# Program order for a product mixed with an attention pass, and a layernorm folded into the weights of the next layer

## The chip, the cores and the metric

The kernel runs on one core of one Trainium2 chip. The metric is device microseconds (us) of one execution; lower is better. Engines are named as in the profile: PE is TensorE, PEld its weight loads, DVE is VectorE, ACT is ScalarE, POOL is GpSimd.

## The reference, cut to what matters

Four graph layers on 4096 nodes with 128 features and one dense 4096x4096 adjacency; after each layer comes a residual sum and a layernorm.

```python
x = _layernorm(x + _L0_gnn_ref(x, adj, ...))   # signed attention
x = _layernorm(x + _L1_gnn_ref(x, adj, ...))   # Chebyshev filter, twice: four products adj @ (4096x128)
x = _layernorm(x + _L2_gnn_ref(x, adj, ...))   # attention with 4 heads of 32
x = _layernorm(x + _L3_gnn_ref(x, adj, ...))   # h @ W_self + (adj @ h / deg) @ W_neigh

# the attention of the third layer
tau = adj_t * exp(max(0.2 * C, C))             # C = alpha_src + alpha_dst, for each pair and head
att = tau / sum(tau)
z   = einsum('mnh,nhf->mhf', adj_t * att, h_prime)
```

The change concerns the fourth product of the Chebyshev layer, the attention, and the layernorm between the attention and the last layer.

## The kernel before: the parts concerned

The attention runs as eight passes (four windows of 1024 target nodes, two pairs of heads) of 32 steps, one step for each tile of 128 source nodes. A step needs three DVE and two POOL instructions and, on PE, two groups of four matmuls with 32 output columns each, one group for the softmax denominator (`den`) and one for the numerator (`num`):

```python
def step(self, nt, l2w, bufs, a, sq):
    E, D = self.E, self.D
    tau  = l2w.tile([P, 2, WB], F32, name="tau",  bufs=bufs[0])
    tau2 = l2w.tile([P, 2, WB], F32, name="tau2", bufs=bufs[1])
    nc.vector.scalar_tensor_tensor(tau[:, 0, :], D[0], E(nt, 0), a, op0=ALU.max, op1=ALU.mult)
    nc.gpsimd.tensor_tensor(tau2[:, 0, OWN:WB], tau[:, 0, OWN:WB], a[:, OWN:WB], ALU.mult)
    nc.vector.scalar_tensor_tensor(tau2[:, 0, 0:OWN], D[0][:, 0:OWN], E(nt, 0), sq, op0=ALU.max, op1=ALU.mult)
    nc.vector.scalar_tensor_tensor(tau[:, 1, :], D[1], E(nt, 1), a, op0=ALU.max, op1=ALU.mult)
    nc.gpsimd.tensor_tensor(tau2[:, 1, :], tau[:, 1, :], a, ALU.mult)
    return tau, tau2

def product(self, is_den, nt, r):
    # ... four matmuls into one accumulator, 32 of its rows each
    for h in range(2):
        for mb in range(2):
            q = 32 * (2 * h + mb)
            nc.tensor.matmul(acc[q:q + 32, :], weights(nt, 2 * self.hp + h, is_den),
                             r[:, h, mb * IB:(mb + 1) * IB], start=nt == 0, stop=nt == NT - 1)
```

The first pass is mixed with the fourth product. There the order on each engine is left to a scheduler:

```python
for ib in range(NB):
    p = ps_p.tile([P, IB], F32, name="pp")
    for c in range(NB):
        a = chunk(ld, adjT, ib, c)
        for k in range(TB):
            nc.tensor.matmul(p, w[:, c * TB + k, :], a[:, k, :], ...)
        if ib >= 2 and done < ready and (c % 2 or ready - done > TB):
            next(first_pass)
            done += 1
    # ... the chain of the block: add, elu, transpose, residual, statistics
    normalize_x(ib, ps_x, "px")
    sources_and_targets(ib)      # ends with four casts to bf16 on DVE
    ready += TB
for heads in first_pass:
    pass
```

The other seven passes stand in a part of the program whose order is kept as written. The last layer's layernorm was explicit, in front of its two products:

```python
nc.vector.tensor_scalar_add(s, mv[:, tb, 1], LN_EPS)
nc.scalar.activation(s, s, AF.Sqrt)
nc.vector.reciprocal(s, s)
nc.vector.scalar_tensor_tensor(m, mv[:, tb, 0], -1.0, s, op0=ALU.mult, op1=ALU.mult)
# eight times:
nc.scalar.activation(r, r, AF.Identity, bias=m[:, k:k + 1], scale=s[:, k:k + 1])
# then transpose, copy, multiply by W3, copy
```

One more line adds the residual to the last layer's own weights, at the very start and on POOL:

```python
nc.gpsimd.tensor_tensor(W3[:, 1, :], W3[:, 1, :], ident, ALU.add)
```

## Time and profile before

The time was 2312.57 us, the median of three runs (2310.97 to 2317.0). The profiled execution has a span of 2316.5 us, so it is one of the slower ones. The stages, by the starts of marker instructions in its trace (the first matmul of the fourth product, DVE's first addition of its last block, DVE's second step of the second pass, ACT's copy of the last `num`):

| stage | from | to | us |
|---|---|---|---|
| layer 0 and three products | 0 | 1100.7 | 1100.7 |
| fourth product, first pass mixed in | 1100.7 | 1420.0 | 319.3 |
| hand-over, up to the second step of the second pass | 1420.0 | 1460.9 | 40.9 |
| seven passes, up to the copy of the last `num` | 1460.9 | 2221.3 | 760.4 |
| tail: last block of the attention, rest of the last product, output | 2221.3 | 2316.5 | 95.2 |

Read such a table by asking, for each row, which engine is full. The lines that show it are in the prediction: PE in the second row, none in the third, DVE in the fourth. A microsecond taken from an engine that is not full in its row is worth nothing by itself.

### The profile page before, as it was taken

The page shows a single profiled execution, that of the slowest core. Times are in us where ns is not written, and L with a number is a line of the kernel's source. Part 1 is how long each engine was busy: PE and PEld are TensorE (multiplying, and loading weights), DVE is VectorE, ACT ScalarE, POOL GpSimd, SP SyncE. Part 2 cuts the span into 40 slices and gives each one's busy share as a digit, 9 for nine tenths or more (in the row PEclk, how much of TensorE's full clock was granted, in tenths as well). Part 3 has the DMA queues.
Part 4 walks back from the last instruction along what each step waited for, and adds up shares of the span by engine and source line. Part 5 has one row for each costly group of instructions (what it writes and reads, how often), then busy time and mean ns, then how long its engine had stood idle before and what let it go on. Part 6 is the DMA issues. An engine that isn't in the chain of part 4 may idle for free. (4 is left out here: it accounts for less than half of the span.)

```text
span 2316.5 us, 22706 instructions
## 1 busy us (share of the span) xinstructions
PE 2189.3 (95%) x8550; PEld 848.2 (37%) x8550; DVE 1235.3 (53%) x1789; ACT 609.3 (26%) x960; POOL 846.3 (37%) x541
## 2 busy tenths in 40 slices
PE   5899999999999999999999998768999999999998
PEld 3333444444444444444433332112222222222233
DVE  5454461000011010000167657899999999999955
ACT  5764100000000000000122121553364335334520
POOL 0000000000000000000043423898999899989930
PEclk9899999999999999999999999999999999999999
DMA  9785758888866767788866774344666566656665
GB/s 370 288 331 202 244 185 281 299 303 297 272 233 236 262 228 260 266 273 273 273 245 226 269 262 175 127 164 146 235 226 233 216 239 237 237 215 238 234 221 180
DMA packets 85336, 561.72 MB, mean 242 GB/s; under 512 B 9568, under 2 KB 15712, under 8 KB 17760
## 3 DMA queue, kind: packets, MB, share of 16 engines
q1 hardware_dynamic: 76928, 554.73, 68.0%
q10 hardware_dynamic: 8288, 5.44, 0.8%
q8 instruction: 69, 1.13, 0.2%
q14 instruction: 51, 0.42, 0.1%
HBM read 558.04 MB, written 2.10 MB: 242 GB/s over the span
## 5 line engine op out<-in xcount | busy, mean ns | idle before, releaser
L647 POOL TENSOR_TENSOR tau<-tau,chunk 128x1024 f32<-128x1024 f32 x256 | 611.0, 2387 | 79.8 <-DVE tau L646 71.8
L659 PE MATMUL den<-tau,cs 128*32 128x512 f32 x2048 | 392.9, 608 | 63.0 <-DVE tau L646 55.4
L601 POOL TENSOR_TENSOR x<-x,B2R 128x512 f32<-128x512 f32 x8 | 10.2, 1270 | 1208.5 <-DMA chunk<-in_adjT 1116.4
L659 PE MATMUL num<-tau,hc 128*32 128x512 f32 x2048 | 374.0, 599 | 4.7 <-POOL tau L647 4.0
L642 DVE SCALAR_TENSOR_TENSOR tau<-d,es,chunk 128x1024 f32<-128x1024 f32 x256 | 326.6, 1276 | 7.4 <-PE d L632 4.1
L646 DVE SCALAR_TENSOR_TENSOR tau<-d,es,chunk 128x1024 f32<-128x1024 f32 x256 | 327.1, 1278 | 0.1
L621 ACT ACTIVATE sq<-chunk 128x704 f32<-128x704 f32 x256 | 200.9, 791 | 410.3 <-DVE tau L644 317.3
L643 POOL TENSOR_TENSOR tau<-tau,chunk 128x320 f32<-128x320 f32 x256 | 226.5, 885 | 64.8 <-DVE tau L642 32.9
L644 DVE SCALAR_TENSOR_TENSOR tau<-d,es,sq 128x704 f32<-128x704 f32 x256 | 241.9, 945 | 13.3 <-PE num L659 9.7
L777 PE MATMUL pp<-chunk,w 128*128 128x512 f32 x512 | 235.6, 601 | 1.2 <-DVE t2T L783 1.2
L731 PE MATMUL pp<-chunk,xT 128*128 128x512 f32 x448 | 236.5, 630 | 0.0
L486 PE MATMUL pacc<-chunk,t 128*128 128x512 f32 x512 | 223.5, 592 | 0.0
L486 PE MATMUL pacc<-chunk,v 128*128 128x512 f32 x512 | 222.5, 592 | 0.0
L486 PE MATMUL pacc<-chunk,x 128*128 128x512 f32 x512 | 221.7, 593 | 0.0
L314 PE MATMUL pacc<-chunk,hw 128*128 128x512 f32 x408 | 197.0, 623 | 2.7 <-DVE hw L379 2.7
L659 PEld LDWEIGHTS den<-tau,cs 128*32 128x32 f32 x2048 | 64.0, 107 | 306.5 <-DVE tau L646 169.8
L659 PEld LDWEIGHTS num<-tau,hc 128*32 128x32 f32 x2048 | 91.3, 110 | 155.0 <-issue 138.3
L486 PEld LDWEIGHTS pacc<-chunk,v 128*128 128x128 f32 x512 | 97.2, 190 | 122.0 <-issue 122.0
L486 PEld LDWEIGHTS pacc<-chunk,x 128*128 128x128 f32 x512 | 96.5, 190 | 117.2 <-issue 117.2
L486 PEld LDWEIGHTS pacc<-chunk,t 128*128 128x128 f32 x512 | 96.1, 190 | 115.3 <-issue 115.3
L777 PEld LDWEIGHTS pp<-chunk,w 128*128 128x128 f32 x512 | 91.7, 190 | 125.8 <-issue 119.0
L533 DVE COPY w<-ptr 128x512 f32<-128x512 f32 x8 | 5.5, 692 | 241.5 <-PE ptr L103 241.5
(182 smaller groups left out, 1574.5 us busy)
## 6 DMA issues: line engine op xcount, KB each, us to landing
chunk<-in_adjT SPq DMA_DIRECT2D x386, 1024.0 KB, 4.9
chunk<-in_adj SPq DMA_DIRECT2D x128, 1024.0 KB, 4.8
keep<-in_adjT SPq DMA_DIRECT2D x13, 1024.0 KB, 5.0
xT<-in_xT ACTq DMA_DIRECT2D x8, 256.0 KB, 6.0
out<-o ACTq DMA_DIRECT2D x8, 256.0 KB, 3.6
W1A<-in_w1a ACTq DMA_DIRECT2D x1, 384.0 KB, 3.5
W1B<-in_w1b ACTq DMA_DIRECT2D x1, 384.0 KB, 4.3
W0T<-in_w0gT ACTq DMA_DIRECT2D x1, 64.0 KB, 5.3
```

What stands on the lines that cost most here:

```text
L314: nc.tensor.matmul(p, hw[:, j * TB + k, :], a[:, k, :], start=first and k == 0, stop=last and k == TB - 1)
L486: nc.tensor.matmul(p, stationary(c * TB + k), a[:, k, :], start=n == 0 and k == 0, stop=n == NB - 1 and k == TB - 1)
L601: nc.gpsimd.tensor_tensor(x[:, tb, :], x[:, tb, :], B2R[:, None, :].to_broadcast([P, TB, F]), ALU.add)
L621: nc.scalar.activation(sq, a[:, 0:OWN], AF.Square)
L642: nc.vector.scalar_tensor_tensor(tau[:, 0, :], D[0], E(nt, 0), a, op0=ALU.max, op1=ALU.mult)
L643: nc.gpsimd.tensor_tensor(tau2[:, 0, OWN:WB], tau[:, 0, OWN:WB], a[:, OWN:WB], ALU.mult)
L644: nc.vector.scalar_tensor_tensor(tau2[:, 0, 0:OWN], D[0][:, 0:OWN], E(nt, 0), sq, op0=ALU.max, op1=ALU.mult)
L646: nc.vector.scalar_tensor_tensor(tau[:, 1, :], D[1], E(nt, 1), a, op0=ALU.max, op1=ALU.mult)
L647: nc.gpsimd.tensor_tensor(tau2[:, 1, :], tau[:, 1, :], a, ALU.mult)
L659: nc.tensor.matmul(acc[q:q + 32, :], weights(nt, 2 * self.hp + h, is_den), r[:, h, mb * IB:(mb + 1) * IB], start=nt == 0, stop=nt == NT - 1)
L731: nc.tensor.matmul(p, y[:, (2 * mp + c) * TB + k, :], a[:, k, :], start=c == 0 and k == 0, stop=c == 1 and k == TB - 1)
L777: nc.tensor.matmul(p, w[:, c * TB + k, :], a[:, k, :], start=c == 0 and k == 0, stop=c == NB - 1 and k == TB - 1)
```

## The change

Its intent: keep the matmul groups of a step together in the mixed stage by writing the order down, let the first pass use the same buffers as the others so that the hand-over closes, and shorten the chain in front of the last product. The diff, cut to its core:

```diff
-    nc.gpsimd.tensor_tensor(W3[:, 1, :], W3[:, 1, :], ident, ALU.add)
+    def later_constants(psum, name):      # called inside layer 0; other constants moved here too
+        ...
+            nc.vector.tensor_tensor(W3[:, 1, :], W3[:, 1, :], ident, ALU.add)
+            nc.vector.memset(mean, 1.0 / F)
+            nc.tensor.matmul(pw, mean, W3..., start=True, stop=True)
+            nc.vector.tensor_sub(W3..., W3..., pw)      # weights without their column mean
 ...
-                nc.vector.tensor_copy(dv[:, blk], d)          # the four casts of the targets
+                nc.scalar.copy(dv[:, blk], d)
 ...
     def layer3_blocks(mp):
-                # statistics, -mean/sigma, eight normalisations, transpose, multiply, copy
+                # transpose x as it is; statistics beside it; multiply; 1/sigma as the copy's scale
+                            nc.scalar.activation(y[:, t, :], q[:, k, 0, :], AF.Copy, scale=scale)
+                            nc.scalar.activation(x[:, t, :], q[:, k, 1, :], AF.Copy, scale=scale)
 ...
-            with tc.tile_pool(name="l2a", ...):   # first pass, own buffers, order left to the scheduler
+            with tc.manual_schedule(engines={PE, DVE, Activation, Pool}):
+                for ib in range(NB):
+                    for c in range(NB):
+                        ...                                   # four matmuls of the fourth product
+                        if c == NB - 1:
+                            chains.append(block_end(ib, p))
+                        one(chains)                           # one segment of a block's chain
+                        if (c in (1, 3, 5, 6, 7) if ib > 2 else (ib, c) == (2, 7)) and ...:
+                            step()                            # one step of the first pass
+                while chains:                                 # the last block's chain between steps
+                    one(chains)
+                    step()
-                    tau, tau2 = heads.step(nt, l2w, (3, 4), a, sq)
+                    tau, tau2 = heads.step(nt, l2w, (3, 3), *ahead)
```

## The prediction

> **What bounds the kernel now.** I read four views in this order: the page's busy shares, the stretches of the run by stage, the order of matmuls inside the overlapped stage, and the vector engine's own order where one stage hands over to the next.
>
> ```profile
> span 2316.5 us, 22706 instructions
> PE 2189.3 (95%) x8550; PEld 848.2 (37%) x8550; DVE 1235.3 (53%) x1789; ACT 609.3 (26%) x960; POOL 846.3 (37%) x541
> ```
>
> The 95% of PE is an average over stages with different limits, so I cut the span by stage. The columns are length, PE, PEld, DVE, ACT, POOL busy, granted clock, DMA share, GB/s.
>
> ```profile
> 1100.00:1420.00 320.00, 316.44 (x1074) 121.42 (x1076) 177.16 (x286) 63.56 (x108) 102.92 (x63) 1.00 0.71 252
> 1420.00:1460.00 40.00, 27.42 (x118) 7.17 (x116) 28.02 (x43) 10.37 (x19) 15.81 (x10) 0.87 0.29 109
> 1460.00:2222.00 762.00, 701.39 (x4085) 200.62 (x4086) 758.33 (x759) 336.62 (x557) 726.45 (x461) 0.99 0.60 214
> 2222.00:2317.00 95.00, 81.32 (x220) 37.45 (x218) 41.69 (x177) 8.68 (x27) 0.00 (x0) 0.93 0.55 188
> ```
>
> Everything before 1100 is layer 0 and three products, PE-bound and hardly touched. Then come: the fourth product with the first attention pass mixed in (PE never idle); a hand-over of 40 us in which no engine is full; seven more passes, bound by DVE (758 of 762 us); and a tail. The change aims at the first two and shortens the chain in the last.
>
> In the mixed stage, the PE order counts. One 128x128 by 512 matmul shows as two records (x2), and four 32-column ones as x8:
>
> ```profile
> 1352.13 1.04 PE L659 MATMUL den<-tau,cs 128*32 128x512 f32 x2
> 1353.11 1.10 PE L591 MATMUL px<-xT,WD 128*96 128x512 f32 x2
> 1354.14 1.04 PE L659 MATMUL den<-tau,cs 128*32 128x512 f32 x2
> 1355.11 1.13 PE L777 MATMUL pp<-chunk,w 128*128 128x512 f32 x2
> 1356.17 1.05 PE L659 MATMUL den<-tau,cs 128*32 128x512 f32 x4
> 1357.15 2.84 PE L777 MATMUL pp<-chunk,w 128*128 128x512 f32 x6
> 1359.92 1.07 PE L659 MATMUL den<-tau,cs 128*32 128x512 f32 x8
> 1360.81 1.05 PE L659 MATMUL num<-tau,hc 128*32 128x512 f32 x8
> ```
>
> Read the starts. A whole group of four takes 0.89 us (1359.92 to 1360.81). But the scheduler split the group of 1352 into 1+1+2: 0.98, 0.97 and 0.98 us, 2.93 in place of 0.89. A whole step, den and num together, takes 1.86 us (1359.92 to 1361.78).
>
> At the hand-over, DVE starts of L642, L644, L646 make one step of pass two:
>
> ```profile
> 1449.72 1.27 DVE L646 SCALAR_TENSOR_TENSOR tau<-d,es,chunk 128x1024 f32<-128x1024 f32 x1
> 1454.40 1.28 DVE L642 SCALAR_TENSOR_TENSOR tau<-d,es,chunk 128x1024 f32<-128x1024 f32 x1 [3.41 <-PE d L632]
> 1458.86 0.95 DVE L644 SCALAR_TENSOR_TENSOR tau<-d,es,sq 128x704 f32<-128x704 f32 x1 [3.17 <-ACT sq L621]
> 1459.73 1.27 DVE L646 SCALAR_TENSOR_TENSOR tau<-d,es,chunk 128x1024 f32<-128x1024 f32 x1
> 1460.92 1.27 DVE L642 SCALAR_TENSOR_TENSOR tau<-d,es,chunk 128x1024 f32<-128x1024 f32 x1
> ```
>
> Two waits of over 3 us for the new pool's buffers and the second pass's targets. From 1460.92 on a step takes 3.24 us of DVE (1.19 + 0.86 + 1.19 start to start) and the engine does not rest again.
>
> **What the Trainium skill says.** "TensorEngine Tiling (Array Packing)", Key Properties: different tiles can load weights and multiply in parallel, and a change of tiling mode drains the engine. The trace agrees on the first: x8 and x4 and x2 all take about 0.9 to 1.0 us. "SBUF — State Buffer", Who interferes with whom: a vector instruction in a two-port mode (casts, copies, tensor_scalar), or one with two SBUF inputs against a reading GpSimd instruction, waits for the whole other instruction. The trace agrees here:
>
> ```profile
> L597 DVE CAST dv<-elu_r x8: 417/2480/2507, 1147.4 to 1440.5; 32x512 bf16<-32x512 f32 x8
> L700 DVE SCALAR_TENSOR_TENSOR mean<-mv,rstd x4: 166/2014/2318, 1596.2 to 2228.6; 128x8 f32<-128x8 f32 x4
> ```
>
> Both (minimum/median/maximum ns) are cheap when GpSimd is idle and take about one 2.4 us GpSimd multiply otherwise. "ScalarE: Activation LUTs", What ACT_TABLE_LOAD costs: about 1283 ns for a load and 93 ns for each pointer operand of an ACTIVATE. The trace has 1283 for the load; the second I need for the new scaled copies.
>
> **The change part by part.** (1) Program order in the mixed stage. Work is the same; the groups of four stay whole (the built order shows den x4, num x4 always together). A block without steps takes 31.24 us before (first matmul sums at 1128.54 and 1159.78), of which 0.85 is a wait for its one accumulator, so 30.4. The last three blocks with four steps each take 42.12, so (42.12 - 30.4)/4 = 2.9 us a step where 1.86 would do. In the new order: block 0 27.7; block 1 30.4; block 2 30.4 + 1.3 for the targets; block 3 30.4 + 8.4 + 1 (5 den, 4 num; 1 for a transposition that waits for the normalisation); blocks 4 to 6 30.4 + 5x1.86 + 1 = 40.7 each; block 7 30.4 + 3x1.86 + 1 = 37.0. The sum is 288.7, so the product ends at 1100.7 + 288.7 = 1389, against 1420. But it holds 24 steps instead of about 28.
>
> (2) The hand-over. Eight steps of the first pass are left, with the last block's chain between them. DVE: 2.7 us to the activation's end and 4.5 to the normalised block (1419.99 to 1422.69 to 1427.19 before), 8x3.24 = 25.9, 1.0 for the products with cs, about 4 for small waits and the next targets. That is 38: the second pass begins at 1427 and its second step at 1431, against 1460.92. Gain of (1) and (2) about 30 us; I take 28, since in program order each chain segment can hold an engine up.
>
> (3) The targets' casts move from DVE to ACT, which has 256 us idle there: inside (1) and (2). The last block's targets are now built in the DVE-bound stage: two subtractions of 0.7 us, each liable to a GpSimd wait, so 2 us lost.
>
> (4) Buffers: tau2 goes from 4 to 3. L644 of step s+1 then needs the num of step s-2. In the steps at 2204 to 2216 that num ends 1.9 to 2.4 us before L644 starts, so it fits, except where a transposition or the two-layer product of the third layer comes in between (1 to 2 us). I charge 3 us.
>
> (5) Layer 3's layernorm. In each of the three inner passes L700 goes (6.3 us of DVE, all on the bound engine); one more rstd addition comes (0.83 us each, 2.5), and the scaled copies are ACT's, with time to spare. I count 1 us of gain, since what waits for GpSimd here is chance.
>
> (6) The tail. Before: x complete at 2224.67, eight statistics 3.2 us, eight normalisations 3.19, then transpose, copy, four products with copies up to 2242.73: 18.1 us. After: transposition and copy 1.7 at once, beside the statistics; per half 1.03 matmul, 1.6 for four scaled copies of 0.4 (as the 0.40 pitch of L704), 0.4 of hand-overs: 3.0; in all 2x(1.7 + 6.0) = 15.4. The chain has also four segments less, so the third product starts four steps earlier and leaves some 4 of its 16 last matmuls less for the tail (3.5 us). PE before was full from 2221 to 2245. Together 4.5 us.
>
> (7) Constants moved into the first 45 us: small DVE instructions, one waiting for W3 near 21 us, beside a DMA-bound start. 1 us lost.
>
> Sum: 28 - 2 - 3 + 1 + 4.5 - 1 = 27.5. 2312.6 - 27.5 = 2285.
>
> **The rivals.** A: the gain is handed back in the DVE-bound stage, because three tau2 buffers tie PE to DVE. For it: PE is busy 701 of 762 us there, and the chain of waits goes through PE for most of those steps. Against: PE catches up every eighth step, when no product piece is issued. If every step lost 0.1 us, 22 us would be gone and the result 2304. B: program order stalls the mixed stage, as PE waits for DVE and ACT at each chain segment, or for a chunk that steps hold longer. For it: six load buffers for two streams. Against: DVE is idle 143 of 320 us there, the DMA share is 0.71 and landing takes 4.9 us at one chunk per 3.5 us. With 3 us a block it would be 2299. C: more than I count: GpSimd waits disappear with L700 and the casts, and the hand-over closes wholly: 2275. A gain over 2% would need 46 us; the stage gives that only if the product and all 32 steps cost no more than their 1.86 and the chains nothing.
>
> **Range and chances.** The main term rests on two durations read directly, so I hold it within 8 us; A and B push up, C down. I give 2273 to 2297 for 8 in 10. Faster by 2% (below 2266) 0.04, within 2% 0.95, slower 0.01.
>
> **What would show it.** The fourth product should end near 1389 with 24 steps done, den always x8. The second pass's step two should start near 1431. From there to the end of the passes should be about 761 us as before, DVE full, L644 without waits for PE num; such waits would be rival A. Waits of PE pp for DMA or for DVE in the mixed stage would be rival B. The tail from the last num to the end should be about 91 us instead of 95. I am wrong if the mixed stage is no shorter, or if it is and the span does not follow.

## The result, and the profile after

After: 2287.76 us, the median of four runs (2287.12 to 2290.74), against 2311.86 (2310.97 to 2317.0) for the kernel before in the same rounds. The ratio is 0.9894, with a 95% interval of 0.9876 to 0.9911: within 2%. A ratio here is the mean time of one kernel's runs over that of the other's of the same rounds, so it is not quite the ratio of the medians. The predicted 2285 us missed by 2.8 us. All outputs are right.

The page's head and the stretches by stage (length; busy time of PE, PEld, DVE, ACT, POOL; granted clock, DMA share, GB/s):

```profile
span 2285.1 us, 22661 instructions
PE 2164.3 (95%) x8552; PEld 848.7 (37%) x8552; DVE 1198.1 (52%) x1764; ACT 623.8 (27%) x996; POOL 843.4 (37%) x540
```

```profile
1108.00:1400.00 292.00, 289.65 (x1003) 120.47 (x1001) 133.63 (x241) 75.66 (x131) 88.37 (x55) 1.00 0.75 269
1400.00:1440.00 40.00, 29.92 (x173) 8.45 (x176) 37.27 (x52) 17.92 (x31) 28.64 (x19) 0.91 0.38 134
1440.00:2198.00 758.00, 705.00 (x4101) 202.31 (x4094) 754.27 (x760) 332.00 (x557) 725.69 (x461) 1.00 0.61 217
2198.00:2285.00 87.00, 76.91 (x218) 36.09 (x218) 41.58 (x178) 8.17 (x29) 0.00 (x0) 0.97 0.58 206
```

PE's 95% is the same as before, and says nothing of where the time went. The rows do: the mixed stage is 292 us, where it was 320; the hand-over is as long as before, but DVE now works for 37.3 of its 40 us, against 28.0; the passes are almost unchanged; the tail is 87 us. And the first boundary has moved the wrong way: the fourth product starts at 1108.0, where it started at 1100.7.

In the mixed stage the groups are whole. PE's order in a block:

```profile
1330.37 1.07 PE L689 MATMUL den<-tau,cs 128*32 128x512 f32 x8
1331.25 1.04 PE L689 MATMUL num<-tau,hc 128*32 128x512 f32 x8
1332.22 3.70 PE L837 MATMUL pp<-chunk,w 128*128 128x512 f32 x8
```

The starts give 0.88 us for `den` and 0.97 for `num`. Blocks that hold five steps take 41.13 us and one without steps 30.85 (from the starts of the blocks' first additions), so a step costs (41.13 - 30.85)/5 = 2.06 us, with its share of the chain. Before it was 2.9.

At the hand-over DVE runs without a pause. Two lines of the targets sit between the steps; 1436.32 is the first step of the second pass and 1439.57 the second:

```profile
1434.30 1.27 DVE L676 SCALAR_TENSOR_TENSOR tau<-d,es,chunk 128x1024 f32<-128x1024 f32 x1
1435.60 0.68 DVE L629 TENSOR_TENSOR elu_r<-elu_r,dv 32x512 f32<-32x512 f32 x1
1436.32 1.28 DVE L672 SCALAR_TENSOR_TENSOR tau<-d,es,chunk 128x1024 f32<-128x1024 f32 x1
...
1439.57 1.27 DVE L672 SCALAR_TENSOR_TENSOR tau<-d,es,chunk 128x1024 f32<-128x1024 f32 x1
```

Set beside the lines of the kernel before in the prediction: the waits of 3.41 and 3.17 us are gone, and eight steps fit where four did.

The waits of DVE and of PE in the seven passes (total us, times, longest us) decide on rival A:

```profile
DVE tau L672 <- POOL tau L673: 1.9, 5, 0.7
```

```profile
PE den L689 <- DVE tau L676: 49.8, 55, 1.0
```

The first is DVE's only entry: DVE never waits for a `num` matmul to give a `tau2` buffer back. PE waits for DVE, not DVE for PE. Three buffers do not tie.

The start of the run is where the surprise lies. Before, POOL waited for the last small constant, W3 (engine, tile and line, releaser; us, times, longest), and had nothing else to do:

```profile
POOL W L83 <- DMA W<-in_w3s: 20.1, 1, 20.1
```

After, the same addition stands in DVE's order, in front of layer 0's masks (`pos`):

```profile
21.27 0.14 DVE L102 COPY att<-ATD 32x1 f32<-32x1 f32 x1
29.85 0.29 DVE L116 TENSOR_TENSOR W<-W,ident 128x128 f32<-128x128 f32 x1 [8.44 <-DMA W<-in_w3s]
30.06 1.22 DVE L327 TENSOR_SCALAR pos<-chunk 128x2048 bf16<-128x2048 f32 x1
```

The bracket says that DVE stood idle for 8.44 us, until the load landed. Nothing behind it in DVE's order could go ahead, and the masks are what layer 0's matmuls eat.

In the tail, the stretch in which the last block's chain runs and its first copies, before (ACT, the normalisations; then the stretch, columns as above) and after:

```profile
2228.83 3.19 ACT L704 ACTIVATE x<-x,mean,rstd 128x128 f32<-128x128 f32 x8 [0.53 <-DVE mean L700]
```

```profile
2229.00:2236.00 7.00, 4.93 (x12) 2.79 (x12) 0.69 (x1) 4.13 (x11) 0.00 (x0) 0.76 0.55 195
```

```profile
2205.54 0.37 ACT L740 ACTIVATE xT<-px,rstd 128x128 f32<-128x128 f32 x1 [1.12 <-PE px L735]
2205.81 0.36 ACT L741 ACTIVATE x<-px,rstd 128x128 f32<-128x128 f32 x1
2206.06 0.37 ACT L740 ACTIVATE xT<-px,rstd 128x128 f32<-128x128 f32 x1
```

```profile
2203.00:2210.00 7.00, 6.32 (x25) 3.81 (x24) 3.20 (x17) 2.98 (x10) 0.00 (x0) 1.00 0.50 184
```

Eight normalisations before took 3.19 us on the chain, 0.40 apart. The scaled copies after start 0.25 to 0.27 us apart. And while PE waited for the chain before, its granted clock fell to a mean of 0.76 over 7 us; in the stretch after it stays at 1.00, because PE is busy for 6.32 of the 7 us. The Trainium skill, "TensorE: Matmul & The Clock Gate", Part 1, puts it so: the default state is throttled and activity releases the throttle. This trace agrees in direction.

By markers, before and after, in the two profiled executions:

| stage | before, us | after, us | gain |
|---|---|---|---|
| up to the fourth product | 1100.7 | 1108.0 | -7.3 |
| fourth product | 319.3 | 292.1 | 27.2 |
| hand-over to the second step of the second pass | 40.9 | 39.5 | 1.4 |
| seven passes | 760.4 | 758.4 | 2.0 |
| tail | 95.2 | 87.1 | 8.1 |
| span | 2316.5 | 2285.1 | 31.4 |

The medians differ by 24.1 us, not by 31.4: the profiled execution of the kernel before is near the slow end of its runs. So a single row is good to a few microseconds only, and most of the parts that matter were run by themselves. Note also that the product's row holds 28 steps before and 24 after, and the hand-over's row 4 and 8.

### The profile page after: what moved, and what is told of

The parts are those of the page before. It is cut to its first block, busy times and chain, and to the rows that moved or that the text cites. A ratio compares the mean times of both kernels' runs of the same rounds, so it can differ in the third digit from the quotient of the medians. Undisturbed runs are those within 1.5% of the kernel's fastest.

```text
span 2285.1 us, 22661 instructions
## 1 busy us (share of the span) xinstructions
PE 2164.3 (95%) x8552; PEld 848.7 (37%) x8552; DVE 1198.1 (52%) x1764; ACT 623.8 (27%) x996; POOL 843.4 (37%) x540
## 5 line engine op out<-in xcount | busy, mean ns | idle before, releaser
L600 POOL TENSOR_TENSOR x<-x,B2R 128x512 f32<-128x512 f32 x8 | 10.3, 1284 | 1183.7 <-PE px L133 1183.7
L689 PE MATMUL den<-tau,cs 128*32 128x512 f32 x2048 | 384.0, 605 | 58.1 <-DVE tau L676 53.6
L689 PE MATMUL num<-tau,hc 128*32 128x512 f32 x2048 | 366.5, 596 | 0.0
L837 PE MATMUL pp<-chunk,w 128*128 128x512 f32 x448 | 202.3, 598 | 0.0
L654 ACT ACTIVATE junk<-chunk 128x1024 bf16<-128x1024 f32 x128 | 133.3, 1042 | 0.0
```

What stands on the lines that cost most here:

```text
L654: nc.scalar.activation(junk, a, AF.Copy, accum_out=deg[:, nt, self.mp:self.mp + 1])
L837: nc.tensor.matmul(p, w[:, c * TB + k, :], a[:, k, :], start=c == 0 and k == 0, stop=c == NB - 1 and k == TB - 1)
```

## The experiments

Three questions were open. Is it the split matmul groups that cost the mixed stage its time (the main step of the prediction)? What do the other parts give when done alone? And is the late start due to the load of W3? My theory is that the groups explain the stage, and that the in-order wait explains the start. The rivals are given with each run. Ten kernels ran, all in three timed rounds. For each, "from the product's start" is its profiled span less the start of its fourth product, which takes the start of the run out of the comparison; it is 1215.8 us before and 1177.1 after.

| kernel | median us (range) | ratio to before (95%) | product starts | DVE waits for W3 | from the product's start |
|---|---|---|---|---|---|
| e1_const_late | 2287.42 (2285.55 to 2289.93) | 0.9883 (0.9865 to 0.9901) | 1107.5 | 10.6 | 1178.0 |
| e2_w3_pool | 2279.77 (2277.76 to 2280.33) | 0.9850 (0.9834 to 0.9867) | 1098.5 | none | 1176.9 |
| e12_w3_early | 2279.86 (2277.87 to 2281.0) | 0.9855 (0.9839 to 0.9872) | 1099.9 | 2.3 | 1177.4 |
| e4_split_den | 2312.45 (2306.05 to 2315.92) | 0.9989 (0.9963 to 1.0015) | 1103.8 | 3.2 | 1204.7 |
| e8_before_norm | 2306.22 (2300.52 to 2309.19) | 0.9968 (0.9951 to 0.9985) | 1096.8 | none | 1201.9 |
| e3_old_norm | 2295.08 (2292.06 to 2298.08) | 0.9914 (0.9897 to 0.9930) | 1110.3 | 9.5 | 1185.5 |
| e6_chain_first | 2284.23 (2281.6 to 2292.69) | 0.9883 (0.9862 to 0.9905) | 1098.2 | none | 1181.1 |
| e10_casts_dve | 2287.62 (2286.63 to 2288.14) | 0.9890 (0.9874 to 0.9907) | 1099.3 | none | 1185.1 |
| e7_more_steps | 2278.25 (2276.79 to 2278.68) | 0.9844 (0.9828 to 0.9861) | 1100.1 | none | 1175.9 |
| e9_consts_pool | 2279.2 (2277.98 to 2280.07) | 0.9849 (0.9832 to 0.9865) | 1100.9 | none | 1176.5 |

The kernel before, beside them, had medians of 2313.26 us (set of e1, e2, e4, e8), 2314.89 (e3, e6, e7, e9) and 2312.55 (e10, e12), seven runs each. Medians of different sets can so be apart by some 2 us for no reason of the kernel. A kernel with four `tau2` buffers, the number before, could not be tried: it does not fit the memory of a partition. A draft of e7 that took 28 steps into the stage read source weights before they were written; it was mended to 26 steps.

### e1_const_late: the moved constants after layer 0 in the source

```diff
-            later_constants(ps_mm, "pmm")          # inside layer 0
+                later_constants(ps_mm, "pmm")      # after the call of layer 0
```

> The changed kernel with the later constants built after layer 0 instead of in its first 60 us. Theory: the changed kernel loses about 7 us at its very start, because the vector engine, which takes its instructions in order, waits 8.44 us for the weight W3 that arrives late behind the adjacency chunks; everything after is shifted. Then the fourth product starts at about 1101 instead of 1108 and the time is about 2281 (2287.8 less 7). Rival: the first 100 us are limited by the transfers anyway, the late start is chance of that one profile, and the time stays at 2287 to 2289.

2287.42 us: nothing gained. But the trace shows that the experiment did not do what its edit says. Layer 0 stands in a part that the scheduler orders, and it moved the addition to the front again: DVE waited 10.6 us for W3. So it tests nothing of the theory, and only teaches that a line's place in the source is not its place in the program there.

### e2_w3_pool: only the addition to W3 on POOL again

```diff
-            nc.vector.tensor_tensor(W3[:, 1, :], W3[:, 1, :], ident, ALU.add)
+            nc.gpsimd.tensor_tensor(W3[:, 1, :], W3[:, 1, :], ident, ALU.add)
```

> The changed kernel with only one instruction moved: the addition of the identity to W3 goes back from the vector engine to GpSimd, which has nothing to do at that time. Theory: this one wait is the whole loss, so 2281 and no vector-engine idle time over 3 us before 30 us. Rival: the small copies that wait for the attention vectors, and the longer queue of constants, cost a part: then 2283 to 2285. If the loss is no wait of the vector engine at all: 2288.

2279.77 us, so 8.0 us less than the changed kernel, by one word. The load was as late as in the changed kernel:

```profile
POOL W L116 <- DMA W<-in_w3s: 29.6, 1, 29.6
```

POOL waited for it until 30.9 us, and nobody waited for POOL. The product starts at 1098.5, and from there on the run is as long as the changed kernel's (1176.9 against 1177.1).

### e12_w3_early: the addition stays on DVE, the load is issued earlier

```diff
     W0 = load_const(w0g, [P, F], "W0")
     # ... eight pieces of xT
+    W3 = const.tile([P, 2, F], F32, name="W3")
+    nc.scalar.dma_start(W3[:, 0, :], w3n)
+    nc.scalar.dma_start(W3[:, 1, :], w3s)
     B1A = load_const(b1a, [P, HH], "B1A")
-    # ... the three W3 lines, behind the other constants
```

> The changed kernel with the two loads of W3 issued ahead of the other small constants, right behind the eight pieces of x transposed; the addition of the identity stays on the vector engine in its place. Theory (the vector engine waits in order for a late load): it is the load's landing that costs, not the engine that adds, so the wait of 8.4 us falls to under 3 us (the attention vectors land about then and are waited for by the same run of instructions), the fourth product starts near 1098 to 1101 as with the addition on GpSimd, and the time is 2279 to 2282. Rival: the addition on the vector engine costs by itself, or the start is bound by the chunk transfers, which the earlier loads push back: 2286 to 2289.

2279.86 us. The wait is shorter:

```profile
17.75 0.29 DVE L116 TENSOR_TENSOR W<-W,ident 128x128 f32<-128x128 f32 x1 [2.33 <-DMA W<-in_w3s]
```

So it was not the engine that cost 8 us, but a late load in front of an in-order engine with other work; either cure is worth the same. The other runs give the same picture unasked. With the addition on DVE, waits of 8.4, 9.5 and 10.6 us go with starts of 1107.5 to 1110.3, waits of 2.3 and 3.2 with 1099.9 and 1103.8, and no wait (e6, where the load happened to land in time) with 1098.2. With it on POOL, the start is 1100.1 where the load landed at 21 us (e7), and 1098.5 and 1099.3 where it landed at 31 (e2, e10).

### e4_split_den: the `den` groups broken into two pairs, with one product matmul between

```diff
-                        heads.product(True, nt, tau)
+                        heads.product(True, nt, tau, (0,) if mixed else (0, 1))   # first pair
+                        if mixed: owed.append(...)     # second pair and num after the next product matmul
```

> The changed kernel, but in the mixed stage each step's four den matmuls are issued as two pairs with one 128-column matmul between them, as the scheduler of the kernel before often had it. Nothing else moves. Theory: a pair takes as long as four, so each of 23 or 24 steps costs 1.0 us more of TensorE, the fourth product takes 24 us longer (ends near 1424 instead of 1400) and the time is about 2310. Rival: the gain came from the hand-over between the pools and from the order of the chains, not from whole groups; then the product ends within 5 us of the changed kernel's and the time is 2288 to 2293.

2312.45 us: by the medians, this alone takes back the whole net gain. From the product's start, which leaves the wait for W3 out, it takes back 27.6 of 38.7 us. The profile is the prediction's reading the other way round:

```profile
1342.68 1.01 PE L133 MATMUL px<-ident,x 128*128 128x128 f32 x4 [0.20 <-DVE x L149]
1343.62 1.05 PE L691 MATMUL den<-tau,cs 128*32 128x512 f32 x4
1344.60 0.70 PE L852 MATMUL pp<-chunk,w 128*128 128x512 f32 x1
```

A pair (x4 in records) takes 0.98 us from start to start, where four took 0.88. The product with its 24 steps took 318.9 us, against 292.1: (318.9 - 292.1)/24 = 1.1 us a step for one more group. The instructions, the buffers and the program order elsewhere were those of the changed kernel, but for `num`, which follows the second pair. (A broken group also means more changes between 32-column and full-width matmuls; this run does not part the two costs.) So in this order the unity of the groups is worth 26.8 us.

That e4 comes out level with the kernel before is in part chance: e4 splits every `den` group, while the scheduler had split only some, but had four steps more in the stage. I summed, in each trace of the stage, the time from every `den` or `num` record of PE to PE's next record. It is 66.4 us before, 41.8 after and 64.1 in e4, and PE came to these matmuls from others 47, 23 and 46 times. The kernel before had some 27.5 groups of `den` and 26 of `num` there; whole, at 0.88 and 0.97 us, they would take 49.4 us. So of the 27.2 us of the product's row, about 17 come from whole groups, about 8 from the four steps that moved into the hand-over, and under 3 from the other matmuls. This split is worked out from traces, not from a run of its own.

### e8_before_norm: the kernel before, with the new layernorm alone

```diff
+            nc.tensor.matmul(pw, mean, W3..., start=True, stop=True)
+            nc.vector.tensor_sub(W3..., W3..., pw)
     def layer3_blocks(mp):      # the new body; the scaled copies
```

> The kernel before with only the new layernorm of layer 3 (centred weights, scaled copies). Theory: it alone gives the shorter tail (95.2 to about 87 us from the last num copy to the end) and removes the 2.1 us vector instruction in each of three passes while adding a 1 us one: 2303 to 2306. Rival: the shorter tail belongs to the new order as a whole and the passes gain nothing: 2310 to 2313.

2306.22 us, ratio 0.9968: 0.0032 of 2313 is 7.4 us. Its passes take 758.0 us and its tail 87.3, the values of the changed kernel to within 0.4 us. So the new layernorm is enough for the gain of the table's last two rows. (The rows that the edit does not touch are 7.5 us shorter than in the trace before: this trace is of its fastest execution, that one of a slow one.)

### e3_old_norm: the changed kernel with the old layernorm

```diff
     def layer3_blocks(mp):      # the old body; no mean taken out of W3
```

> The changed kernel with the old layernorm of layer 3 put back (normalise first, then transpose; weights not centred). Theory from the run of the layernorm alone: the tail goes back from 87 to about 95 us and the passes grow by about 2 to 3 us, so 2297 to 2299, and the two parts of the change add up. Rival: in the new order the freed vector and scalar time is of no use, because other waits cover it: 2288 to 2291.

2295.08 us, 7.3 more than the changed kernel's median; from the product's start, 8.4 more. The time lies below the 2297 to 2299 that were expected. Its passes are 3.0 us longer than the changed kernel's, but its tail, at 92.3 us, gives back only 5.2 of the 8.1 us; what keeps the other 3 was not isolated. By the medians the layernorm is worth about 7 us with and without the rest of the change, so the parts add to within the scatter.

### e6_chain_first: the last block's chain ahead of the remaining eight steps

```diff
                 while chains:
                     one(chains)
-                    step()
```

> The changed kernel with the last block's chain run to its end before the remaining eight steps of the first pass, instead of a step after each segment. Theory: the hand-over term is the hiding of that chain; it has about 5 to 6 us beyond the normalisation (transposition, copy, two products, exponentials), in which the vector engine then stands: second step of the second pass 5 to 7 us later, 2293 to 2295. Rival: TensorE and the scalar engine hold the steps up to the same time anyway: 2288 to 2290.

The whole time, 2284.23 us, missed its expectation and is lower than the changed kernel's. But the start is the reason: W3 landed in time in the profiled execution, and the product started at 1098.2. Measured from its start, this kernel is 4.0 us longer than the changed one. Its hand-over, from the product's end to the second step of the second pass, is 43.6 us, against 39.5, and DVE shows why:

```profile
1400.74 0.49 DVE L612 TENSOR_TENSOR hc<-px,cs 128x128 f32<-128x128 f32 x2 [2.77 <-ACT es L609]
1402.91 0.49 DVE L612 TENSOR_TENSOR hc<-px,cs 128x128 f32<-128x128 f32 x2 [1.68 <-ACT es L609]
```

The chain's links to PE and ACT leave DVE idle for 4.5 us when no steps lie between them. So the theory holds when measured from the product's start, at a smaller size than expected: that part of the change is worth about 4 us.

### e10_casts_dve: e2 with the four casts of the targets on DVE again

```diff
-                nc.scalar.copy(dv[:, blk], d)
+                nc.vector.tensor_copy(dv[:, blk], d)
     # and the other three casts alike
```

> The version with the W3 addition on GpSimd (2279.8 us), with the four casts of the attention targets on the vector engine again, as before the change. Theory (step 3 of the prediction: the move is worth something only where the vector engine is the bound): seven of eight blocks' casts lie in the mixed stage, where the vector engine is idle about half the time, and cost nothing; the last block's four lie after it, at 0.42 us each when GpSimd is idle and about 2.4 us when it multiplies, so 2 to 8 us more: 2282 to 2288, and it shows between the first targets of the last block and the second pass. Rival 1: the casts were worth much more, as they hold the vector engine at each chain segment of the mixed stage, and the product itself gets longer than 292 us by over 8 us: 2290 or more. Rival 2: on one engine the chain of cast, subtract, cast needs no hand-over to ScalarE, and that pays for the casts: 2278 to 2281.

2287.62 us, 7.9 more than e2. Seven of the eight blocks lie in the mixed stage, where DVE has time. The last one lies where DVE is full, and its casts meet POOL's multiplications:

```profile
1420.20 2.32 DVE L623 CAST dv<-elu_r 96x512 bf16<-96x512 f32 x1 [0.41 <-ACT elu_r L622]
...
1426.40 2.46 DVE L626 CAST dv<-elu_r 32x512 bf16<-32x512 f32 x1
1428.88 0.42 DVE L627 CAST dv<-elu_r 32x512 bf16<-32x512 f32 x1
...
1433.41 2.46 DVE L630 CAST dv<-elu_r 32x512 bf16<-32x512 f32 x1
```

2.32 + 2.46 + 0.42 + 2.46 = 7.66 us, the loss to within 0.3 us of the medians' 7.9. The theory of the cost held, at the top of its range, and it shows that this move of work off DVE is worth what it takes in the stage where DVE is full, and nothing elsewhere: the product took 292.1 us as in e2. The Trainium skill, "SBUF — State Buffer", Who interferes with whom, says that casts can contend with GpSimd and that the later of the two then waits for the whole instruction of the other. The trace agrees: the casts took 0.42 us free and 2.32 to 2.46 us when they met POOL's multiplications, whose mean is 2.39 us.

### e7_more_steps and e9_consts_pool: looking for a better version

e7 is e2 with 26 steps in the mixed stage. e9 is e7 with the constants that layer 0 doesn't need loaded from POOL's queue.

```diff
-   (c in (1, 3, 5, 6, 7) if ib > 2 ...) and ... < min(ready, NT - 2 * TB)
+   (c in (1, 2, 3, 5, 6, 7) if ib > 2 ...) and ... < min(ready, NT - TB - 2)
```

> The W3 addition on GpSimd, and two more first-pass steps placed in the fourth product (26 in place of 24, six to a block). Theory: a step costs about 2.1 us of TensorE in the product and 3.24 us of the vector engine after it, so each of two is worth 1.1 us: 2277 to 2278 against 2279.8. Rival: six steps in a block hold TensorE up, as their den comes before the vector engine is done: 2281 to 2285.

```diff
+        eng = nc.scalar if name in ("W0T", "A0", "W0") else nc.gpsimd
-        nc.scalar.dma_start(t, src)
+        eng.dma_start(t, src)
```

> The kernel with 26 steps, and the constants that are not needed at the start are fetched from GpSimd's queue instead of the scalar engine's. Theory: the scalar engine's first real instruction came at 18.6 to 19.7 us because it was issuing these fetches; if it starts near 11 us, layer 0 starts up to 7 us earlier: 2271 to 2274. Rival: the first 60 us are limited by the adjacency transfers (DMA share 0.9 and more), so nothing is gained: 2277.

e7 took 2278.25 us, the lowest median, at the upper edge of its expectation: its ratio to before is 0.9844. It is not clear of e2 and e9 by more than the scatter. Nearly all of that is e2's word; the two more steps gave 1 us from the product's start, which is inside what one trace can tell. e9 was no faster (2279.2): ACT waited 13.9 us in place of 18.4 before its first work, and the product's start stayed at 1100.9. The Trainium skill, "DMA: Bandwidth & Descriptors", Issuing engines are not separate DMA queues, says that transfers run on the same 16 DMA engines whoever started them, and that another issuing engine saves only issue time. These runs agree: nothing was gained.

## Why the prediction was right or wrong, point by point

The time and the class were right: 2287.8 against 2285, inside the range. The sum holds errors of opposite sign: by the traces the first three rows below were put 10.3 us too low, and step (7) was put 6.3 us too cheap. That the number came within 2.8 us is in part luck. In the terms of the prediction, with what the profiled pair and the experiments show:

| term | predicted gain, us | measured, us | shown by |
|---|---|---|---|
| (1) to (3) mixed stage, hand-over, casts | 28 - 2 = 26 | 28.7 (product's start to second step of second pass: 360.2 to 331.5) | traces; e4, e6, e10 |
| (4) and (5) three buffers, layernorm inside the passes | -3 + 1 = -2 | 2.0 (760.4 to 758.4) | traces; e8 |
| (6) tail | 4.5 | 8.1 (95.2 to 87.1) | traces; e8, e3 |
| (7) constants at the start | -1 | -7.3; by medians -8.0 | e2, e12 |

- Steps (1) and (2) held in mechanism, and in size as a sum: the product was put at 288.7 us and took 292.1, the hand-over to the second step at 42 and took 39.5. The block of no steps was put at 30.4 and took 30.8 to 30.9, the block of five at 40.7 and took 41.1, the last at 37.0 and took 39.1. The second pass's second step came 331.5 us after the product's start; the prediction's 1431 meant 330.3. e4 shows what whole groups are worth, and e6 that the interleaved chain is about 4 us. That the waits of 3.41 and 3.17 us went because the first pass shares its buffers with the others is seen in the traces alone; no run isolates it.
- Step (3) held. The last block's two subtractions took 0.68 us each. That the casts had to go to ACT to get it is what e10 shows.
- Step (4) was too careful: no wait for `num` in 758 us. Rival A is refuted by the list of waits; how four buffers would do here stays untried.
- Step (5) was right in its items: the instruction at L700 went, 6.3 us, and the additions for 1/sigma grew from 2.5 to 6.2 us, six at a mean of 1036 ns. That nets 2.6 us, for the 1 that was counted; the passes as a whole gained 2.0.
- Step (6) had the right parts at the wrong size. From the complete x to the last copy it took 13.9 us (2202.2 to 2216.1), with 15.4 predicted and 18.1 before. The error is the "four scaled copies of 0.4": that pitch was taken from an instruction with two pointer operands. The page cited in the prediction, "ScalarE: Activation LUTs", What ACT_TABLE_LOAD costs, also gives an immediate ACTIVATE as 186 ns plus 0.833 ns an element, and an overlap of about 93 ns back to back. An estimate with one pointer from that page is 186 + 93 + 0.833 x 128 - 93 = 293 ns; the trace has 0.25 to 0.27 us. I had also put the previous window's matmuls left for the tail at 16, with four fewer after the change; there were 8 and then 5, at 0.86 us each. "PE before was full from 2221 to 2245", for which the sum was cut to 4.5, was a wrong reading: PE was busy for 21.9 of these 24 us, at a mean clock of 0.93. And the clock that fell while PE waited was not in the sum at all.
- Step (7) is the one that failed: "small DVE instructions, one waiting for W3 near 21 us, beside a DMA-bound start. 1 us lost." The 21 us came from the trace before, where the load was issued at 19.4 us and landed at 21.4, just when the other operands of that code were there. I took the landing time of a load as fixed. It is not: in the changed kernel, 11.4 us passed from issue to landing, and the in-order DVE stood for 8.44 of them. e2 and e12 each take that back for 8 us.
- Rivals. A fell as said. B, stalls of the mixed stage, fell: PE's only listed wait between 1108 and 1400 is 2.4 us in total, for the normalised x. C, more than counted, was nearer the truth of the stages: without step (7)'s wait, the change is at 2279.8.

Left open: why the load of W3 landed 3 us after its issue in some executions and over 11 in others of the same code at the start (e7 and e2, for instance). Loads of 1 MB chunks were under way at the same time, but no run here took those away.

## What to carry to other kernels

Before an instruction is moved to another engine, look at what it waits for as well as what it costs: a wait of 20 us on an idle engine is free, and the same wait in the order of a busy one holds up all that is behind it. When small matmuls share PE with large ones, count groups, not matmuls: keep those that can run side by side together, and check in the order of starts that the scheduler has done so. And work out the price of a move by stage: the same four casts cost nothing in seven blocks and 7.7 us in the eighth.

## What the Trainium skill lacked or had wrong

- "TensorEngine Tiling (Array Packing)", Key Properties, says that tiles run in parallel and that a change of mode drains the engine, but gives no cost for a group that is broken up. Here four 32-column matmuls of 512 take 0.88 us from start to start and a pair 0.98 us; breaking 24 groups into pairs around one full-width matmul cost 26.8 us, or 1.1 us each.
- "ScalarE: Activation LUTs", What ACT_TABLE_LOAD costs: its figures give an estimated pitch of 293 ns for a 128-column copy with one pointer scale. The scaled copies here read PSUM and start 0.25 to 0.27 us apart (0.36 to 0.38 us each), somewhat faster. The page does not say where the input of its tiles lies, and no run here tests whether that is the reason.
- "DMA: Bandwidth & Descriptors" has no figure for how late a small load becomes behind large ones. The same 64 KB load landed from 1.9 us (the kernel before) to 12.7 us (e2) after its issue.
